# Clustering stage of an attention and cluster block: another order of the one-hot steps, and the table load moved ahead of the filler

## The chip, the cores and the metric

The kernel runs on one core of a Trainium2 chip. A core has five engines that run beside each other, each working through its own list of instructions in order: TensorE (PE in the profile, with its weight loads as PEld), VectorE (DVE), ScalarE (ACT), GpSimd (POOL) and SyncE (SP), which only starts DMA transfers here. They wait for one another by semaphores. The metric is the time of one execution on the device, in microseconds (us). Everything is computed in fp32.

## The reference

Two layers are applied to x of shape (4, 256, 64, 64): a self-attention over the 4096 positions of each image, and then a block with a group norm, a clustering, an MLP and two batch-normed products. The change lies in the clustering alone:

```python
feat, val = conv1x1(x, f_w, f_b), conv1x1(x, v_w, v_b)   # 96 channels: 4 heads of 24
xf, vf = split(feat), split(val)        # image folded 2 x 2, heads apart
cen, v_cen = pool(xf), pool(vf)         # 4 centres for each fold and head
cn, pn = cen / |cen|, pts / |pts|
sim = sigmoid(beta + alpha * cn @ pn.T)             # 4 centres x 1024 points
mask = one_hot(argmax(sim, over the centres))       # each point keeps its best centre
sim = sim * mask
agg = (sim @ v2 + v_cen) / (mask.sum(-1) + 1)
out = sim.T @ agg                                   # back to the points
```

The kernel takes the sigmoid as 0.5 tanh(half the argument) + 0.5. So for each point: a length, a scaled product, a tanh, an affine step, and a one-hot of the largest of four values, the first one where two are equal.

## The kernel before, in words

The four images are handled one after the other: attention, clustering, MLP. Their work is interleaved: while the clustering or the MLP of one image waits, matmuls of the next image's projections (or, for the last image, the rest of the one before) are put in as filler. `fill(n)` takes n such pieces from a list; a piece `v_half` is two matmuls (L314, tile vp), and after each second one ScalarE copies the result out (L322). The order on each engine is the order of the Python program: nothing is reordered afterwards.

In `cluster`, an image is cut into 8 blocks of 512 points. For each block `nb`, PE computes features, values and scaled similarities in one group of matmuls (L861, tile fv). VectorE then copies out features and values with their bias (L870, tile vf) and the similarities (L877, tile sg), and the squares of the features (L841, on GpSimd but for the last block) are summed to lengths (L842, tile prn, in `heads`).

Blocks 0 to 3 make the first row of folds, blocks 4 to 7 the second, and `f` is 0 or 1 for them. When all lengths of a row are there, `similar(f)` takes the reciprocal root (L171 on VectorE, the root L172 on ScalarE, the reciprocal L174 on VectorE), scales the similarities with it (L812, VectorE) and takes the tanh (L813, ScalarE). `largest(f)` has the affine step (L821), the largest of four (L822), a comparison (L823) and a product with a rank (L824), and `weights(f)` the largest rank (L830), the one-hot (L831) and the product of similarity and one-hot (L834, tile sim). The table `later` says where the first row's steps stand: `similar(0)` ahead of block 6, and `largest(0)` and `weights(0)` ahead of block 7, whose copies L870 and L877 thus follow them on VectorE.

ScalarE needs another function table for the root than for the tanh. `table(f)` runs one small activation on a tile `probe` (L237), by which the table is loaded at that place. In `similar` this stands behind the whole of `rsqrt`, and with it behind whatever `meanwhile` puts in: for the second row `fill(2)`, a filler piece whose copy L322 is then ahead of the load on ScalarE.

After the last block PE runs `fill(2)`, then 32 small matmuls with the pooling weights (L891, agg from pool_w), which need the values of every block, then the filler of `similar(1)` and `fill(3)`. Then it counts the points of each centre with matmuls over the one-hots (L912, tile cnt), sums the weighted values (L891, agg from sim), turns sim and the sums (L930, L939) and multiplies with the projection (L951, tile gp). The last image has its filler from the MLP of image 2's last block (L1059, L1076), with tanh-based activations of it (L1071, in `gelu`) behind each tanh.

Of the kernel before, what the change touches and what calls it, by code (L numbers as in the profile page):

```python
# [9 lines left out]
AF = mybir.ActivationFunctionType  # L10
ALU = mybir.AluOpType
AX = mybir.AxisListType
# [14 lines left out]
L2_EPS = 1e-12  # L27
# [18 lines left out]
def attention_then_cluster_block(  # L46
# [17 lines left out]
    nc = tc.nc  # L64
# [104 lines left out]
    def rsqrt(dst, src, eps, meanwhile=lambda: None):  # L169

        nc.vector.tensor_scalar(dst, src, eps, None, ALU.add)  # L171
        nc.scalar.activation(dst, dst, AF.Sqrt)  # L172
        meanwhile()
        nc.vector.reciprocal(dst, dst)  # L174
# [60 lines left out]
    def table(f):  # L235

        nc.scalar.activation(probe, probe, f)  # L237
# [455 lines left out]
    def cluster(b, ys, stats, cells, rest, fill, gelu):  # L693
# [51 lines left out]
        bests = [scr[:, f * 64 : (f + 1) * 64] for f in range(2)]  # L745
# [3 lines left out]
        oh = scr[:, NB:]  # L749
# [22 lines left out]
        for f, o in enumerate((0, 16 + 2 * ED)):  # L772
# [15 lines left out]
        prns = [small.tile([P, 64], F32, tag="prn", name=f"prn_{b}_{f}") for f in range(2)]  # L788

        sgs = [  # L790
            work.tile([P, NB // 2], F32, tag=f"w{f}", bufs=1, name=f"sg_{b}_{f}") for f in range(2)
        ]

        sim = spool.tile([P, 8, 4, 32], F32, tag="s", name=f"sim_{b}")
# [3 lines left out]
        def folded(t):  # L798
            return t.rearrange("p (q j s) -> p q j s", q=2, j=8)

        def quad(t):
            return t.rearrange("p (c m) -> p c m", m=4)

        def over_m(t):
            return t.unsqueeze(2).to_broadcast([P, 64, 4])

        def similar(f, meanwhile=lambda: None):

            sg = sgs[f]
            rsqrt(prns[f], prns[f], L2_EPS, meanwhile)  # L810
            table(AF.Gelu_apprx_tanh)
            nc.vector.tensor_tensor(quad(sg), quad(sg), over_m(prns[f]), ALU.mult)  # L812
            nc.scalar.activation(sg, sg, AF.Tanh, scale=ab[:, 0:1], bias=ab[:, 1:2])  # L813
            if f == 0:
                gelu(0)
                table(AF.Sqrt)

        def largest(f):

            sg, o, best = sgs[f], oh[:, f * 256 : (f + 1) * 256], bests[f]  # L820
            nc.vector.tensor_scalar(sg, sg, 0.5, 0.5, ALU.mult, ALU.add)  # L821
            nc.vector.tensor_reduce(best, quad(sg), AX.X, ALU.max)  # L822
            nc.vector.tensor_tensor(quad(o), quad(sg), over_m(best), ALU.is_equal)  # L823
            nc.vector.tensor_tensor(  # L824
                quad(o), quad(o), rank.unsqueeze(1).to_broadcast([P, 64, 4]), ALU.mult
            )

        def weights(f):
            sg, o, best = sgs[f], oh[:, f * 256 : (f + 1) * 256], bests[f]
            nc.vector.tensor_reduce(best, quad(o), AX.X, ALU.max)  # L830
            nc.vector.tensor_tensor(quad(o), quad(o), over_m(best), ALU.is_equal)  # L831
            own = slice(2 * f, 2 * f + 2)
            s = sim[:, :, own, :16].rearrange("p j q s -> p q j s")
            nc.vector.tensor_tensor(s, folded(sg), folded(o), ALU.mult)  # L834
        later = {6: lambda: similar(0), 7: lambda: (largest(0), weights(0))}

        def heads(nb):

# [10 lines left out]
        for nb in range(NBLK):  # L849
            fh, o = nb // 4, nb % 4  # L850
# [17 lines left out]
            for g in range(2):  # L868
                q = 2 * fh + g
# [30 lines left out]
        summed(lambda j, q: pool_w[:, j], True)  # L900
        heads(NBLK - 1)
        similar(1, lambda: fill(2))
        gelu(1)
        fill(3)
        table(AF.Sqrt)
        largest(1)
        weights(1)

        cnt_p = ps_a.tile([P, NB], F32, tag="a1", name=f"cnt_{b}")
# [632 lines left out]
    with tc.manual_schedule():  # L1542
        here = attention(0, xs0)
        here.alone()
        late = None
        for b in range(B):
            xs1, begun = [], []
            nxt = attention(b + 1, xs1) if b + 1 < B else None

            def ahead():  # L1550
                if nxt and len(xs1) < N // XT:
                    xs1.append(load_x(b + 1, len(xs1)))
                elif late and not begun:
                    begun.append(begin())

            begin, todo, gelu = late or (None, list(nxt.projections) if nxt else [], lambda i: None)
            fill = filler(todo)
            stats, cells, rest = here.weighting(ahead, fill, (lambda: None) if b else derived)
            turned = turn_w2(b, not nxt)
            stats2 = cluster(b, here.xs, stats, cells, rest, fill, gelu)  # L1560

            late = mlp(b, here.xs, stats2, fill, nxt, NBLK - (b == B - 2), turned)
            here = nxt
# [76 lines left out]
```

## Time and profile before

| | |
|---|---|
| median of 3 runs | 3378.88 us (3378.66 to 3379.28) |
| the profiled execution: its own time | 3378.26 us |
| its span, first to last instruction | 3376.5 us |
| PE, DVE, ACT, POOL busy | 98%, 66%, 50%, 57% of the span |
| mean granted clock of PE | 0.996 of full speed |
| the chain that ended last | PE 94%, DVE 4%, ACT 1% |

The profile is of one execution; times within it are us from the first instruction. A busy share is time in which an engine had an instruction running. The granted clock is the share of its full speed at which PE was allowed to run. The chain that ended last is followed back from the last instruction, at each step to what released it or to the instruction before it on its engine. A view of waits puts an engine's idle time down to the instruction that released it. In all views L12 is line 12 of the kernel.

### The profile page before, as it was taken

To read this page: it belongs to the slowest core of one execution; us is meant where nothing else is said; L and a number is where in the kernel's file an instruction comes from. 1 tells how busy PE (TensorE), PEld (TensorE's weight loads), DVE (VectorE), ACT (ScalarE), POOL (GpSimd) and SP (SyncE) were. 2 spreads that over 40 slices of the span, in tenths; PEclk is the share of its full clock that TensorE was granted. 3 is DMA by queue.
4 is the path that set the end of the run, shared out by engine and by line. 5 is a ranking of instruction groups with operands and counts; after the bars stand their busy time and mean duration, and the time that the engine had idled before them with its cause. 6 is when DMAs were issued, how large, how long until landed. Compare 5 with 4: busy or idle time off the path is not lost.

```text
span 3376.5 us, 34772 instructions
## 1 busy us (share of the span) xinstructions
PE 3318.5 (98%) x12322; PEld 1815.5 (54%) x12322; DVE 2226.3 (66%) x3546; ACT 1687.1 (50%) x2253; POOL 1929.7 (57%) x1366
## 2 busy tenths in 40 slices
PE   8999999999999999999999999999999999999999
PEld 4434445788533444578843334457873344346686
DVE  5667664677666766467766676646766766764675
ACT  5545543445555554345555555434555555544444
POOL 2655666366365666536645566554644676573664
PEclk9999999999999999999999999999999999999999
DMA  2000002000000000100000000020000000010000
GB/s 71 13 13 11 16 7 86 4 13 19 25 13 13 13 13 22 70 4 19 14 29 13 10 13 13 22 71 4 20 26 13 13 13 13 10 39 1 13 20 26
DMA packets 43102, 70.99 MB, mean 21 GB/s; under 512 B 9680, under 2 KB 18480, under 8 KB 42928
## 3 DMA queue, kind: packets, MB, share of 16 engines
q1 hardware_dynamic: 38064, 61.94, 5.5%
q10 hardware_dynamic: 4608, 6.30, 0.8%
q8 instruction: 97, 1.59, 0.2%
q14 instruction: 77, 0.63, 0.1%
q0 software_dynamic: 256, 0.52, 0.1%
HBM read 43.46 MB, written 16.89 MB: 18 GB/s over the span
## 4 chain that ended last, share of the span: by engine, by line
PE 94%; DVE 4%; ACT 1%; POOL 0%; issue 0%; DMA 0%; SPq 0%; ACTq 0%; POOLq 0%; DVEq 0%
PE av L477 53%; PE mo L1278 10%; PE sc L363 8%; PE hq L1361 5%; PE hp L1361 3%; PE hr L1361 3%; PE vp L314 2%; PE fv L861 2%; PE mo L1262 1%; PE hq_pw L1361 1%; PE pw L1215 1%; PE hr_pw L1361 1%; PE op L982 1%; PE hp_pw L1361 1%; PE qp L333 0%; PE kp L291 0%
## 5 line engine op out<-in xcount | busy, mean ns | idle before, releaser
L477 PE MATMUL av<-s,v 128*128 128x512 f32 x4096 | 1819.2, 598 | 0.6 <-ACT s L467 0.6
L472 POOL TENSOR_TENSOR acc<-acc,s 128x1024 f32<-128x1024 f32 x448 | 1057.1, 2360 | 538.3 <-ACT s L467 519.5
L477 PEld LDWEIGHTS av<-s,v 128*128 128x128 f32 x4096 | 759.0, 190 | 1044.8 <-issue 1034.5
L467 ACT ACTIVATE s<-s 128x1024 f32<-128x1024 f32 x512 | 541.0, 1059 | 591.1 <-DVE s L464 550.2
L464 DVE TENSOR_TENSOR s<-s,mb 128x1024 f32<-128x1024 f32 x512 | 595.8, 1206 | 18.4 <-ACT mb L448 16.7
L385 DVE TENSOR_TENSOR top<-sc,top 128x1024 f32<-128x1024 f32 x196 | 239.4, 1222 | 374.7 <-PE sc L363 374.6
L1316 ACT ACTIVATE hs<-hs,pv_s 128x256 f32<-128x256 f32 x496 | 233.3, 505 | 339.2 <-DVE hs L1352 339.2
L1278 PE MATMUL mo<-hs,w 128*128 128x256 f32 x1512 | 387.9, 382 | 0.0
L381 ACT COPY s<-sc 128x1024 f32<-128x1024 f32 x224 | 225.1, 1005 | 225.6 <-PE sc L363 225.6
L1278 PEld LDWEIGHTS mo<-hs,w 128*128 128x128 f32 x1512 | 282.0, 190 | 60.2 <-ACT hs L1316 19.9
L363 PE MATMUL sc<-q,k 32*128 32x512 f32 x2048 | 299.9, 640 | 0.4 <-ACT s L386 0.4
L388 DVE TENSOR_TENSOR top<-sc,top 128x1024 f32<-128x1024 f32 x196 | 240.1, 1225 | 72.6 <-ACT s L381 59.6
L386 ACT COPY s<-sc 128x1024 f32<-128x1024 f32 x224 | 227.3, 1015 | 66.0 <-DVE top L383 36.1
L1352 DVE TENSOR_TENSOR hs<-hq,hs 128x256 f32<-128x256 f32 x496 | 198.5, 421 | 75.5 <-PE hq L1361 65.2
L469 POOL TENSOR_TENSOR acc<-s 128x1024 f32<-128x1024 f32 x32 | 75.3, 2352 | 287.6 <-ACT s L467 287.6
L1285 POOL TENSOR_TENSOR hs<-hs 128x256 f32<-128x256 f32 x108 | 82.3, 762 | 194.5 <-ACT hs L1369 91.4
L363 PEld LDWEIGHTS sc<-q,k 32*128 32x128 f32 x2048 | 86.4, 182 | 183.1 <-issue 122.0
L1352 DVE TENSOR_TENSOR hs<-hp,hs 128x256 f32<-128x256 f32 x124 | 52.1, 420 | 143.0 <-ACT hs L1369 143.0
L1361 PE MATMUL hr<-xn,w 128*128 128x256 f32 x496 | 127.5, 379 | 0.5 <-DVE hs L1352 0.5
L314 PE MATMUL vp<-wv_s,x 128*128 128x256 f32 x512 | 123.4, 387 | 0.2 <-ACT v L322 0.2
L314 PEld LDWEIGHTS vp<-wv_s,x 128*128 128x128 f32 x512 | 93.5, 190 | 25.5 <-issue 10.5
L1361 PEld LDWEIGHTS hr<-xn,w 128*128 128x128 f32 x496 | 94.1, 190 | 19.1 <-issue 4.8
(261 smaller groups left out, 3528.0 us busy)
## 6 DMA issues: line engine op xcount, KB each, us to landing
x<-in_x SPq DMA_DIRECT2D x32, 512.0 KB, 6.7
out<-xn SPq DMA_DIRECT2D x62, 256.0 KB, 2.1
w<-in_w SPq DMA_DIRECT2D x8, 1024.0 KB, 10.7
mr<-row_mx SPq DMA_DIRECT2D x28, 256.0 KB, 3.1
rden<-row_rd SPq DMA_DIRECT2D x28, 256.0 KB, 3.1
q<-q ACTq DMA_DIRECT2D x96, 64.0 KB, 2.0
mix<-in_wfv SPq DMA_DIRECT2D x8, 192.0 KB, 8.4
q<-q SPq DMA_DIRECT2D x24, 64.0 KB, 2.1
```

The lines of the kernel that those rows point to most:

```text
L314: nc.tensor.matmul(vps[0][:, i % 2, :], xs[i * P // XT][:, k, o : o + P], wv_s[:, k, :], start=(k == 0), stop=(k == KC - 1),)
L363: nc.tensor.matmul(halves[r // 2][:, r % 2, :], k_s[rows, g, :], q_s[rows, :], start=True, stop=True)
L385: nc.vector.tensor_tensor(top, halves[1], top, ALU.max)
L388: nc.vector.tensor_tensor(top, halves[0], top, ALU.max)
L464: nc.vector.tensor_tensor(sh, sh, mxs[nb].unsqueeze(1).to_broadcast([P, 2, NB]), ALU.subtract)
L467: nc.scalar.activation(sh, sh, AF.Exp)
L472: nc.gpsimd.tensor_tensor(acc, acc, s[:, 2 * h : 2 * h + 2], ALU.add)
L477: nc.tensor.matmul(av[c], own["v"][:, RG * g + quarter, c * P : (c + 1) * P], slots[u][:, quarter, :], start=(g == 0 and quarter == 0), st ...
L1278: return nc.tensor.matmul(bank[:, half * HB : (half + 1) * HB], a[:, j], t, start=start, stop=stop)
L1316: nc.scalar.activation(src, src, AF.Gelu_apprx_tanh, bias=pvc("b1", P, j + 4 * (i > 1)))
L1352: nc.vector.tensor_tensor(dst, ps, term, ALU.add)
L1361: nc.tensor.matmul(out, w, x, start=True, stop=True)
```

## The change

`largest` and `weights` are cut anew. The affine step becomes a function of its own, `affine(f)`. `largest(f)` now goes up to the one-hot, and `weights(f)` has only the last product. Ahead of block 7 there is only `affine(0)`. The first row's one-hot comes after `similar(1)`, its filler and its table loads in the program; on VectorE it follows the scaling of the second row's similarities directly. Then come the second row's affine step and one-hot, and at the end both products. In `similar`, the table of the tanh is asked for between the root and the filler of `meanwhile`.

```diff
-            rsqrt(prns[f], prns[f], L2_EPS, meanwhile)
-            table(AF.Gelu_apprx_tanh)
+            def between():
+                table(AF.Gelu_apprx_tanh)
+                meanwhile()
+
+            rsqrt(prns[f], prns[f], L2_EPS, between)
...
+        def affine(f):
+            nc.vector.tensor_scalar(sgs[f], sgs[f], 0.5, 0.5, ALU.mult, ALU.add)
+
         def largest(f):
             sg, o, best = sgs[f], oh[:, f * 256 : (f + 1) * 256], bests[f]
-            nc.vector.tensor_scalar(sg, sg, 0.5, 0.5, ALU.mult, ALU.add)
             nc.vector.tensor_reduce(best, quad(sg), AX.X, ALU.max)
             nc.vector.tensor_tensor(quad(o), quad(sg), over_m(best), ALU.is_equal)
             nc.vector.tensor_tensor(
                 quad(o), quad(o), rank.unsqueeze(1).to_broadcast([P, 64, 4]), ALU.mult
             )
-
-        def weights(f):
-            sg, o, best = sgs[f], oh[:, f * 256 : (f + 1) * 256], bests[f]
             nc.vector.tensor_reduce(best, quad(o), AX.X, ALU.max)
             nc.vector.tensor_tensor(quad(o), quad(o), over_m(best), ALU.is_equal)
-            own = slice(2 * f, 2 * f + 2)
-            s = sim[:, :, own, :16].rearrange("p j q s -> p q j s")
-            nc.vector.tensor_tensor(s, folded(sg), folded(o), ALU.mult)
-        later = {6: lambda: similar(0), 7: lambda: (largest(0), weights(0))}
+
+        def weights(f):
+            s = sim[:, :, 2 * f : 2 * f + 2, :16].rearrange("p j q s -> p q j s")
+            nc.vector.tensor_tensor(
+                s, folded(sgs[f]), folded(oh[:, f * 256 : (f + 1) * 256]), ALU.mult
+            )
+
+        later = {6: lambda: similar(0), 7: lambda: affine(0)}
...
         gelu(1)
         fill(3)
         table(AF.Sqrt)
+
+        largest(0)
+        affine(1)
         largest(1)
+        weights(0)
         weights(1)
```

## The prediction

> **What bounds the kernel now.** I read the page first: TensorE (PE) is busy 98% of the span, and the chain that ended last is 94% PE and 4% VectorE (DVE). A change on VectorE and ScalarE (ACT) can matter only where PE waits for them. So next the waits of PE over the whole run (engine, line and what it waited for: us in total, times, longest):
>
> ```profile
> PE cnt L912 <- DVE scr L831: 9.9, 4, 2.7
> ...
> PE agg L891 <- DVE vf L870: 2.1, 8, 0.3
> ```
>
> The first row is PE's longest wait of all, and the diff reorders the very instruction named, L831, the last step of the one-hot. It occurs once per image: 2.71 us in images 0, 1, 2 and 1.74 in image 3. The second row is the copy-out of the last features. Then the chain through image 1's wait (start us, length us, what):
>
> ```profile
> 1450.06 0.65 DVE sg L821
> ...
> 1453.44 0.47 DVE vf L870
> ...
> 1454.01 0.47 DVE vf L870
> 1454.48 0.04 issue
> 1454.53 0.52 PE agg L891 x10
> 1455.04 1.94 PE vp L314 x8
> 1457.00 0.59 ACT v L322
> 1457.61 1.28 ACT L237
> 1458.90 0.20 ACT probe L237
> 1459.11 0.50 ACT sg L813
> ...
> 1462.26 2.82 PE cnt L912 x16
> ```
>
> The chain winds through three engines: the first row's one-hot (L821 to L834) delays the last features (L870), these delay the pooling matmuls (L891) and the filler matmuls behind them (vp), the filler's copy (L322) stands ahead of the table load, the load ahead of the tanh (L813), and the second row's one-hot comes last. The timeline has the idle times (start, length, what, idle before it and its releaser):
>
> ```profile
> 1454.97 4.58 PE L314 MATMUL vp<-wv_s,x 128*128 128x256 f32 x20
> 1462.26 2.82 PE L912 MATMUL cnt<-scr,ones 128*96 128x64 f32 x16 [2.71 <-DVE scr L831]
> ...
> 1457.22 0.42 DVE L812 TENSOR_TENSOR sg<-sg,prn 128x256 f32<-128x256 f32 x1
> 1459.63 0.29 DVE L821 TENSOR_SCALAR sg<-sg 128x256 f32<-128x256 f32 x1 [1.99 <-ACT sg L813]
> ```
>
> VectorE idles 1.99 us for the tanh just when PE is about to run out of filler. Last, busy time by stretches of 3.41 us, laid on the moments at which PE's granted clock changes (each engine's busy us and count, then the clock, DMA share, GB/s):
>
> ```profile
> 1458.64:1462.05 3.41, 0.92 (x5) 0.46 (x3) 2.25 (x6) 2.90 (x6) 0.00 (x0) 1.00 0.00 0
> 1462.05:1465.47 3.42, 3.21 (x28) 3.09 (x32) 0.90 (x4) 0.00 (x0) 0.00 (x0) 0.50 0.00 0
> 1465.47:1468.88 3.41, 3.41 (x66) 3.12 (x59) 0.67 (x2) 0.24 (x1) 0.00 (x0) 0.50 0.00 0
> ```
>
> PE was busy 0.92 us of the first stretch, and its clock is 0.50 in the next two: the wait is paid a second time, as slow matmuls behind it.
>
> [...] all drops and returns lie on one grid of 3.413 us (625.75, 1462.05, 2301.7, 3114.1), [...] stretches with PE busy 0.70, 0.92, 1.38 and 1.67 us (the four counting waits) were followed by half clock, stretches with 1.76 (from 3144.80) and 1.82 us (from 1492.77) were not. [...] the load here is 1283 ns, but the probe starts 0.02 us after it, so I use 1.28 + 0.20. [...]
>
> **The change, part by part (image 1; images 0 and 2 have the same intervals within 0.02 us).**
> 1. Six DVE instructions (L822, L823, L824, L830, L831, L834) leave the place ahead of the last L870. They stand at 0.457 us start to start, and move L870 from 1453.36 to about 1450.73. It cannot go earlier: its matmuls (L861) end about 1450.7, the earlier blocks being copied out every 2.82 us (1442.25, 1445.07). The affine L821 stays put; its end, 1450.70, falls together with that. Gain 2.63 us for everything on DVE up to L812: 1457.22 becomes 1454.59. GpSimd's square for the block before (L841, until 1450.42) is ready.
> 2. The pooling matmuls no longer wait. 52 of 64 records took 1.35 us, so all take 1.66, from 1452.31 to 1453.97, where the filler began at 1454.97: 1.00 us earlier. Filler then ends at 1458.55 instead of 1459.55, its first copy L322 starts at 1456.00.
> 3. The table load follows the square root. The root starts at 1456.34 - 2.63 = 1453.71 (the copy ahead of it ends at 1453.01), load and probe until about 1455.4, before PE delivers: the 1.48 us are hidden behind the matmuls. The tanh now waits only for the copy: 1456.50, against 1459.01. If that cover were gone, the tanh would lose up to 1.5 us.
> 4. Five DVE instructions of the first row come in behind L812: 1454.59 + 0.46 + 5 x 0.457 = 1457.34. The tanh lets DVE go at 1456.50 + 0.62 (1459.01 to 1459.63 before) = 1457.12. So DVE is now last, by 0.2 us. Affine and five steps take 1459.63 to 1462.26 = 2.63 before, hence counting starts at 1459.97: **2.29 us earlier**, and PE's wait is 1.42 us.
> 5. The two weight products (2 x 0.46) go behind the one-hots; counting takes PE at least 1.55 us, which hides them. Nobody else waits for them. No DMA, no SP or GpSimd instruction moves.
> Image 3 has no copy ahead of the tanh: L812 at 3108.66 - 2.63 = 3106.03, first row done at 3108.78, which replaces 3110.09: 1.31 us, wait 1.44. Sum of the shifts: 3 x 2.29 + 1.31 = **8.2 us**.
> 6. The clock. With at most 1.44 us idle, a stretch keeps at least 1.97 us busy, above the edge between 1.67 and 1.76, so half clock should vanish from the four places. From counting to the gp matmul (L951) it took 5.76, 7.23, 5.73, 5.73 us. At full clock: counting 1.55 (2300.32 to 2301.87), 64 records of agg 1.66 (as in 2), then 1.22 (629.74 to 630.96 of image 0): 4.43. Savings 1.33 + 2.80 + 1.30 + 1.30 = **6.7 us**. Unknown is whether small matmuls count as busy: if they do not, this is 0; if they do, 6.7. I take 6.7, because at half clock the stretch 625.75 to 629.16, made of counting and agg alone, brought the clock back.
> Sum 14.9 us. Against the profiled execution (3378.26, span 3376.5) that is 3363.4; the runs' median is 0.6 above, so 3364.0.
>
> **Rivals.**
> A (forecast): both terms, **3364.0**, own range 3361.5 to 3367.5; 0.50.
> B: the shift comes, but the clock falls in most places, since the stretch around the wait holds mostly 64-column matmuls. For it: image 3's stretch had only 1.74 us idle, and 1.38 of its 1.67 busy were counting. Against it: the return at 629.16. 3378.9 - 8.2 = 3370.7, with partial cases from 3367.5; 0.27.
> C: the filler does not come earlier (the pooling has another floor), so copy at 1457.00, tanh 1457.50, DVE 1458.12: 1.51 x 3 + 1.31 = 5.8 us, clock still falling: 3373.1, or 3372 to 3378 with further losses; 0.15. That the reordering does nothing is part of it: against it, L831 is named on PE's chain.
> D, the other side: the same grid bites elsewhere. At the start of each MLP PE idles in short pieces (stretch from 1492.77: busy 1.82, barely above the edge), and at the end of the attention hand-over (busy 1.98 from 2533.80). Everything behind moves against the grid. A stretch that falls costs up to 1.7 us, half of 3.41. To end slower than before under B's 8.2 us, five such stretches must fall; eleven places at most would give 3378.9 - 8.2 + 18.7 = 3389. Three runs within 0.62 us speak against such swings; 0.08 together with what I overlooked.
>
> **How the numbers follow.** Likeliest is A. The range reaches from 3361.0 (0.4 us per image more, from DVE slots that close up) to 3373.0, taking in A, B and the upper part of C; some 0.2 is left out. A measurement of this kernel tells about 0.2%, 6.8 us: faster is below 3372.1 (A, B, a little of C, 0.80), the same up to 3385.6 (most of C and part of D, 0.14), slower 0.06.
>
> **What would show it.** Right: L870 of the last block starts about 0.0 us after its matmuls; no PE wait at pooling; in images 0 to 2 the table load starts within 0.05 us of the root; DVE has no idle before the second affine; PE waits 1.4 us for counting, 5.7 in sum instead of 9.9; granted clock 1.00 behind it; counting to gp 4.4 us. Wrong: an idle DVE before the second affine (then the copy is the floor, C), a clock of 0.50 behind counting (B), or new half-clock stretches in the MLP starts (D).

## The result, and the profile after

The changed kernel takes 3362.7 us (median of 6 runs, 3361.72 to 3363.63) against 3379.05 us (6 runs, 3377.62 to 3379.28): ratio 0.9953, 95% interval 0.9944 to 0.9963, or 16 us. The forecast was 3364.0, range 3361.0 to 3373.0. The profiled execution took 3361.72, with a span of 3359.9 us against 3376.5.

In the view of PE's waits over the whole run, the row that led the list has moved to third place:

```profile
PE kp L291 <- DMA x<-in_x: 9.7, 3, 8.7
PE tt L399 <- DVE top L393: 7.0, 3, 3.9
PE cnt L923 <- DVE scr L834: 5.4, 4, 1.4
```

The counting (L912 before, L923 now) waits 5.4 us instead of 9.9 in sum. The row of the pooling matmuls waiting for the last features, 2.1 us before, is gone altogether.

The chain through image 1's wait (start us, length us, what) is now VectorE alone, but for one root:

```profile
1446.82 0.55 DVE vf L877
...
1449.58 0.20 DVE prn L171
1449.79 0.02 issue
1449.81 0.27 ACT prn L172
1450.07 0.02 issue
1450.10 0.56 DVE prn L174
1450.66 0.02 issue
1450.68 0.43 DVE sg L816
1451.11 0.34 DVE scr L828
...
1452.85 0.42 DVE scr L834
1453.27 0.21 DVE sg L823
...
1455.33 0.43 DVE scr L834
1455.77 0.04 issue
1455.81 1.57 PE cnt L923 x16
```

The copy-out of the last features (L877, before L870) follows the affine step L823 at once. Filler, filler's copy, table load and tanh have left the chain. The timeline of the same place (start, length, what; PE, then ScalarE, then VectorE) shows where they went:

```profile
1448.44 1.53 PE L898 MATMUL agg<-vf,pool_w 128*32 128x96 f32 x64
1449.89 4.58 PE L314 MATMUL vp<-wv_s,x 128*128 128x256 f32 x20
1455.81 1.57 PE L923 MATMUL cnt<-scr,ones 128*96 128x64 f32 x16 [1.33 <-DVE scr L834]
...
1450.08 1.28 ACT L237 ACT_TABLE_LOAD   x1
1451.38 0.20 ACT L237 ACTIVATE probe<-probe 128x1 f32<-128x1 f32 x1
1451.92 0.58 ACT L322 COPY v<-vp 128x512 f32<-128x512 f32 x1 [0.34 <-PE vp L314]
1452.41 0.60 ACT L817 ACTIVATE sg<-sg,ab 128x256 f32<-128x256 f32 x1
...
1453.19 0.28 DVE L823 TENSOR_SCALAR sg<-sg 128x256 f32<-128x256 f32 x1
```

All pooling matmuls (32 instructions, which show as 64 records) run without a gap. The load is over before PE delivers the filler that ScalarE copies, the tanh follows, and the second affine has no idle time ahead of it, where it had 1.99 us. Last, the stretch of the clock's grid in which image 1's wait lies and the next (busy us and count of PE, PEld, DVE, ACT, POOL, then the granted clock):

```profile
1452.60:1456.01 3.41, 2.08 (x11) 1.52 (x10) 3.20 (x10) 2.48 (x4) 0.00 (x0) 1.00 0.02 5
1456.01:1459.42 3.41, 3.41 (x86) 3.19 (x86) 1.41 (x5) 0.24 (x1) 0.00 (x0) 1.00 0.00 0
```

The clock stays at 1.00. From counting to the gp matmul it takes 4.18 us in every image.

Two intervals that can be read in any trace of this kernel serve for all that follows, image by image: S, from the end of the last L861 group (L868 after) to the start of counting, holds the shift; K, from counting to the gp matmul, holds the clock.

| kernel | S, images 0 to 3 | PE's wait | K, images 0 to 3 |
|---|---|---|---|
| before | 11.61, 11.61, 11.61, 10.62 | 2.71 x 3, 1.74 | 5.76, 7.22, 5.73, 5.73 |
| after | 9.03, 9.03, 9.04, 9.03 | 1.33 to 1.37 | 4.18, 4.19, 4.18, 4.19 |

S falls by 3 x 2.58 + 1.59 = 9.3 us and K by 24.45 - 16.74 = 7.7 us, together 17.0; the spans differ by 16.6. The remaining 0.4 lies outside S and K. The largest piece of it is ahead of them: in image 0 the last L868 group ended at 614.17 us where the last L861 group had ended at 613.59. This point lies between 613.59 and 614.97 in the twelve traces of this document, so a difference of 0.6 us there is within the scatter of single executions.

### The profile page after: what moved, and what is told of

The parts are those of the page before. It is cut to its first block, busy times and chain, and to the rows that moved or that the text cites. A ratio compares the mean times of both kernels' runs of the same rounds, so it can differ in the third digit from the quotient of the medians.

```text
span 3359.9 us, 34780 instructions
## 1 busy us (share of the span) xinstructions
PE 3308.0 (98%) x12322; PEld 1807.2 (54%) x12322; DVE 2225.8 (66%) x3546; ACT 1683.6 (50%) x2253; POOL 1930.0 (57%) x1366
## 3 DMA queue, kind: packets, MB, share of 16 engines
q8 instruction: 97, 1.59, 0.2%
## 4 chain that ended last, share of the span: by engine, by line
PE 94%; DVE 5%; ACT 1%; issue 0%; POOL 0%; DMA 0%; SPq 0%; ACTq 0%; POOLq 0%; DVEq 0%
PE av L477 53%; PE mo L1289 10%; PE sc L363 8%; PE hq L1372 5%; PE hp L1372 3%; PE hr L1372 3%; PE vp L314 2%; PE fv L868 2%; PE mo L1273 1%; PE hq_pw L1372 1%; PE pw L1226 1%; PE hr_pw L1372 1%; PE op L993 1%; PE hp_pw L1372 1%; PE qp L333 0%; PE kp L291 0%
```

## The experiments

All ratios are to the kernel before, measured on the same chip beside it. Line numbers are each kernel's own.

**Without the table move.** The reordering alone:

```diff
-            rsqrt(prns[f], prns[f], L2_EPS, between)
+            rsqrt(prns[f], prns[f], L2_EPS, meanwhile)
+            table(AF.Gelu_apprx_tanh)
```

> The changed kernel with the table load put back behind the filler: only the reordering is left. Theory 1 (the shift and the clock both count): in images 0 to 2 the tanh again waits for copy, load and probe, 1.48 us more, VectorE idles about 1.3 us before the second affine, PE's wait for counting becomes about 2.7 us and the clock falls to 0.50 behind it. Time 3362.7 + 3 x 1.35 + 3 x (1.3 to 2.8) = 3370.7 to 3375. Theory 2 (shift alone counts, the clock costs nothing): 3362.7 + 4.1 = 3366.8. Theory 3 (the table move is hidden by the filler): 3362.7.

Measured: 3368.86 us, ratio 0.9973 (0.9963 to 0.9983). The timeline of image 1, ScalarE and then VectorE:

```profile
1454.72 0.58 ACT L322 COPY v<-vp 128x512 f32<-128x512 f32 x1 [1.86 <-PE vp L314]
1455.33 1.28 ACT L237 ACT_TABLE_LOAD   x1
1456.62 0.20 ACT L237 ACTIVATE probe<-probe 128x1 f32<-128x1 f32 x1
1456.73 0.59 ACT L813 ACTIVATE sg<-sg,ab 128x256 f32<-128x256 f32 x1
...
1457.35 0.29 DVE L819 TENSOR_SCALAR sg<-sg 128x256 f32<-128x256 f32 x1 [1.28 <-ACT sg L813]
```

S is 10.4 in images 0 to 2 and 9.03 in image 3: the mechanism as expected, 1.37 us an image, with VectorE idle for 1.28. So the load is not hidden by the filler (theory 3 falls). PE's wait is 2.71 us again, and K is 5.61, 7.07, 4.19, 4.19. That image 2 kept its clock behind a wait of 2.71 us was not expected. The traced execution is the slowest of the eight, 3371.30 us, and lies inside theory 1's 3370.7 to 3375; six of the others lie between 3368.46 and 3369.30, below it. The median is 6.2 us above the changed kernel's 3362.7, and the shift takes 4.1 of that; the 2 us left are less than two falls of the clock at 1.4 us each (5.61 against 4.19), where three had been expected (by the ratios it is 6.8 us in all, and the same holds). Which images kept the clock in those runs was not traced.

**The table move alone**, in the kernel before: the edit to `similar` of the change and nothing else.

> The kernel before with the table load alone moved ahead of the filler. Theory 1: the root still comes late, so load and probe end at 1458.0 of the old timeline, one us after the filler's matmuls; the tanh gains only 0.5 us in images 0 to 2 and nothing in image 3, PE's wait stays at 2.2 us and the clock still falls: 3379.0 - 1.5 = 3377.5. Theory 3 (the load is what the tanh waited for): 3 x 1.48 and full clock, about 3379.0 - 4.4 - 5.4 = 3369.

Measured: 3374.99 us, ratio 0.9991 (0.9984 to 0.9997), a gain of 3.0 us (1 to 5.4). S fell by 0.51 in images 0 to 2 and by less than 0.01 in image 3, as worked out: the root comes so late in the old order that load and probe end at 1457.96, when the filler has long been delivered (its copy started at 1457.00 in the kernel before). Nearly all of the rest is the clock: image 1 lost one half-clock stretch instead of two (K 5.73, not 7.22). The expectation had left that out, and the time is lower by it. So alone the parts bring 3.0 us and, from the run before, about 9; together 16. Together they bring more than the sum, since only the early root lets the load end before the filler (in image 1 of the changed kernel load and probe end at 1451.58, and the copy starts at 1451.92), and only both bring all four waits to 1.4 us.

**The clock alone.** Matmuls that nobody reads fill PE's wait in the kernel before:

```diff
         cnt_p = ps_a.tile([P, NB], F32, tag="a1", name=f"cnt_{b}")
+        for _ in range(3 if b == B - 1 else 5):
+            nc.tensor.matmul(
+                cnt_p[:, C:], wv_s[:, 0, :P], wv_s[:, 1, :], start=True, stop=True
+            )
```

> The kernel before, with matmuls that nobody reads put into PE's wait for counting: five of 128x256 (about 2.3 us) in images 0 to 2, three (1.4 us) in image 3. Counting starts when it did, so the shift is nil and only the clock is changed. Theory 1: granted clock 1.00 behind the wait, counting to gp 4.4 us instead of 5.7 to 7.2, time 3379.0 - 6.7 = 3372.3. Theory 2 (the clock costs nothing on this path): 3379.0 or a little more.

Measured: 3371.27 us, ratio 0.9979 (0.9971 to 0.9988): 7.1 us faster by adding work. Image 1 on PE:

```profile
1459.11 2.32 PE L911 MATMUL cnt<-wv_s 128*128 128x256 f32 x10
1461.98 1.57 PE L916 MATMUL cnt<-scr,ones 128*96 128x64 f32 x16 [0.55 <-DVE scr L831]
1463.48 1.53 PE L891 MATMUL agg<-vf,sim 128*32 128x96 f32 x64
```

S is 11.60 to 11.61 and 10.62, the same as before; K is 4.18 to 4.19 in all images. The counting matmuls take 1.57 us (2.82 before), the sums 1.53 (2.79 before). The clock is thus a cost of its own, and it makes 7.1 of the 16 us; what is left, 9.3, is the fall of S.

**The control.** The changed kernel with two such matmuls in its shorter wait.

> The changed kernel with two such unread matmuls (0.9 us) in its shorter wait of about 1.35 us in each image. The control of the run before: if the shorter wait already keeps the clock up, they change nothing, 3362.7; if some clock was still lost, or if busy matmuls help or hurt in another way, the time moves by over 1 us.

Measured: 3362.68 us, ratio 0.9953 (0.9938 to 0.9968), S and K as in the changed kernel. Nothing is left to be had from the clock there, and in these four runs (3361.68 to 3363.64) the added matmuls show no other effect.

**How much room is left.** One or two extra VectorE reductions between the first row's one-hot and the second affine, in the changed kernel; the second kernel has `range(2)` in place of `range(1)`:

```diff
         largest(0)
+        for _ in range(1):
+            nc.vector.tensor_reduce(bests[0], quad(oh[:, :256]), AX.X, ALU.max)
         affine(1)
```

> The changed kernel with one extra VectorE reduction, whose result nobody reads, between the first row's one-hot and the second affine: counting 0.46 us later in each image, PE's wait about 1.8 us. Theory 1 with the edge at 1.7 us idle in a stretch of 3.41: 3362.7 + 1.8 = 3364.5 where the wait is split by the grid, and up to 1.3 us more for each image where it is not, at most 3370. Theory 2 (no cost of the clock): 3364.5.

> The same with two extra reductions: counting 0.91 us later, PE's wait about 2.3 us. Theory 1: 3362.7 + 3.7 = 3366.4, and the clock falls in most images, 1.3 us or more each: 3370 to 3373. Theory 2: 3366.4, twice the step of one reduction and no kink.

One: 3363.07 us, ratio 0.9959 (0.9945 to 0.9972); S 9.48 to 9.49, wait 1.79 to 1.82, K 4.18 to 4.19 in all images. Two: 3367.44, ratio 0.9975 (0.9964 to 0.9986), with runs up to 3374.76; S 9.94, wait 2.24 to 2.27, K 4.18, 4.18, 5.77, 4.18. Each reduction moves counting by its 0.46 us at once: VectorE does set the start of counting. With one the clock held everywhere, which both theories allowed at 3364.5, so this run doesn't tell them apart. Theory 1's edge of 1.7 us idle was my estimate from stretches of the kernel before (1.74 us idle lost the clock, 1.65 kept it). With two it fell, in the traced execution, in one image only, and four of the seven runs are lower than the 3370 to 3373 of theory 1. The other three (3370.15 to 3374.76) were not traced.

**When the clock falls.** Theory 1 had expected more falls than came. Between the first 20 and the last 8 us of the kernel before, the granted clock goes to 0.50 at 625.77, 1462.03, 2301.71, 2540.64, 3114.08 and 3137.98 us and comes back 3.41 or 6.83 us later; in that of the changed kernel it goes at 2527.80 and 3121.72. All these moments lie multiples of 3.413 us apart within each trace, and so do the falls worked out from stretches of 0.2 us in four experiments (reordering alone: 626.58, 1459.43, 2534.63; table move alone: 626.74, 1463.01, 2299.28, 3111.64; one reduction: 2528.54, 3122.46; two: 2292.26, 2531.19, 3128.52, 3135.35). Below, the first line of each pair is a stretch of this grid, the second the one after, whose granted clock (the third number from the end) shows whether it fell. The kernel before, image 3:

```profile
3110.69:3114.10 3.41, 1.67 (x17) 1.38 (x16) 2.26 (x6) 2.93 (x5) 0.00 (x0) 1.00 0.00 0
3114.10:3117.52 3.42, 3.42 (x70) 3.03 (x69) 0.99 (x3) 0.24 (x1) 0.00 (x0) 0.50 0.02 5
```

One extra reduction, image 0:

```profile
620.49:623.90 3.41, 1.62 (x10) 1.11 (x9) 3.20 (x10) 2.07 (x3) 0.00 (x0) 1.00 0.00 0
623.90:627.31 3.41, 3.41 (x86) 3.19 (x86) 1.30 (x4) 0.29 (x2) 0.00 (x0) 1.00 0.02 5
```

The reordering alone, image 0 and then image 2:

```profile
623.17:626.58 3.41, 1.99 (x40) 1.92 (x44) 2.28 (x7) 0.73 (x2) 0.00 (x0) 1.00 0.00 0
626.58:630.00 3.42, 3.42 (x60) 3.13 (x50) 0.82 (x3) 0.68 (x2) 0.00 (x0) 0.50 0.02 5
...
2295.70:2299.11 3.41, 2.25 (x52) 2.19 (x56) 2.31 (x7) 0.46 (x2) 0.00 (x0) 1.00 0.00 0
2299.11:2302.52 3.41, 3.38 (x57) 2.58 (x45) 0.61 (x3) 1.74 (x4) 0.00 (x0) 1.00 0.02 5
```

With 1.67 us busy the clock fell, with 1.62 it held. In the last two PE ran counting and sums alone: behind 1.99 us busy the clock fell, behind 2.25 it held. So no single edge of busy time fits the stretches as they are cut here. And a wait of 2.71 us that the grid cuts into 1.55 and 1.16, as in image 2 here (1.86 and 2.25 us busy), was harmless in both halves.

The stretches differ in what PE ran: of the 1.67 us, 1.38 were counting, and of the 1.62, 1.32 were filler of 256 columns. Why the clock fell behind the one and held behind the other, no run here shows.

A wait of 1.33 us followed within its stretch by counting and sums alone would leave 2.08 us busy (an estimate, 3.41 less 1.33). That lies between 1.99, where the clock fell, and 2.25, where it held, and what the clock would do is open. No image of the changed kernel lay so in its trace: the stretches with the waits had 2.05 to 2.12 us busy, most of it filler.

**A step further.** In the changed kernel VectorE idles 0.32 us for the root and is last by 0.16 us. The first edit issues the tanh ahead of the filler's copy, the second also puts the first row's first reduction into the wait for the root:

```diff
-        similar(1, lambda: fill(2))
+        similar(1, lambda: top(0))
+        fill(2)
```

The diff shows the second edit, without the lines that make the first reduction of `largest(f)` a function `top(f)`; the first edit has `similar(1)` instead.

> The changed kernel itself once more, to stand beside the next two on one chip: ratio 0.9953 to the kernel before.

> The changed kernel with only the tanh issued ahead of the filler's copy on ScalarE. In the changed kernel VectorE reaches the second affine last, 0.16 us after the tanh would let it go, so an earlier tanh is worth nothing: the same time within 0.5 us, and PE's wait stays at 1.33 us. If the filler's copy were the floor (rival C), counting would come up to 0.9 us earlier in images 0 to 2.

> A try at more: the first row's first reduction put between the second row's square root and its reciprocal, where VectorE idles 0.32 us, and the tanh issued ahead of the filler's copy on ScalarE. VectorE sets the start of counting, so it comes 0.3 us earlier in each image: 3362.7 - 1.3 = 3361.4. If the filler's copy or the tanh were the floor instead, the gain in images 0 to 2 would be over 0.5 us each or nothing.

> The kernel with the first row's first reduction in VectorE's wait for the root and the tanh ahead of the copy, beside the changed kernel on one chip. From its trace counting comes 0.45 us earlier in each of four images: 1.8 us faster than the changed kernel, ratio 0.9947 to 0.9948 to the kernel before.

Side by side: the changed kernel 3362.62 us, ratio 0.9955 (0.9942 to 0.9969); the tanh first 3361.47, 0.9952 (0.9940 to 0.9965); with the reduction 3360.74, 0.9950 (0.9937 to 0.9962), and on another chip 3359.91, 0.9947 (0.9934 to 0.9959). The tanh alone leaves S at 9.03 to 9.04 and PE's wait at 1.34 to 1.37, so the copy was not the floor; the ratios don't tell these two apart. With the reduction, S is 8.58 in all four images, 0.45 less. VectorE:

```profile
1449.64 0.20 DVE L171 TENSOR_SCALAR prn<-prn 128x64 f32<-128x64 f32 x1
1449.75 0.41 DVE L823 TENSOR_REDUCE scr<-sg 128x64 f32<-128x256 f32 x1
1450.16 0.55 DVE L174 RECIPROCAL prn<-prn 128x64 f32<-128x64 f32 x1
```

The reduction fits into the wait and the reciprocal follows without idle. Beside the changed kernel all five runs (3360.02 to 3361.17) lie below all five of its (3361.43 to 3364.12). The medians differ by 1.9 us, where 1.8 were expected, though the intervals of the ratios overlap. From the kernel with the tanh alone the median differs by 0.7 us only. Between the first and the last counting its trace is 1.54 us shorter than that kernel's, where 3 x 0.45 = 1.35 were to come; but its first counting started 0.26 us later, since the work ahead of S had ended 0.73 us later.

## Why the prediction was right, step by step

**Step 1, the last features earlier: right.** L877 starts 0.04 us after the modelled end of its matmuls (1446.78 to 1446.82).

**Step 2, the pooling: right, a little small.** 64 records took 1.45 us to the start of the filler, not 1.66 (the 1.35 us of 52 records from which 1.66 was scaled up run to the modelled end of the last one; here that end, 1449.97, lies 0.08 us behind the start of the next matmul, 1449.89), so the filler came 1.21 us earlier against the end of the last features' matmuls instead of 1.00.

**Step 3, the load behind the root: right, and the experiments show that it carries its part.** The estimate of 1.5 us if its cover were gone measured 1.37 us an image with the move undone.

**Step 4, VectorE last: right in kind, 0.28 to 0.29 us too small in each image.** VectorE goes on to the second affine without idle, with 0.16 us to spare (0.2 forecast). The forecast shift was 2.29 and 1.31, measured 2.58 and 1.59. Most of it is the term of the slots: I took 0.457 us for every step. Two instructions that don't need their predecessor's result started 0.34 to 0.35 us after it, L828 behind L816 (1450.68 to 1451.03) and the affine behind the one-hot (1452.85 to 1453.19). That is 0.23 us. The prediction had named it, "DVE slots that close up", only for the lower end.

**Step 5, the products behind: right.** Both end at 1456.42, while counting runs until 1457.38.

**Step 6, the clock: right in size and in outcome, but its reason is not secured.** 6.7 us were forecast, K fell by 7.7; the run with filled waits has 7.1. Too small was the gain, since 4.43 was taken for K at full clock and 4.18 measured; of the 0.25 the sums are most, 1.46 us from their start to the next matmul against the 1.66 taken over from step 2. The sentence that a stretch with 1.97 us busy lies safely above an edge between 1.67 and 1.76 does not hold for stretches cut as the prediction cut them: one with 1.99 us busy, all of it small matmuls, fell. The edge was my estimate from the kernel before, and the experiments show no such edge: 1.62 us busy kept the clock, 1.99 lost it. The waits of 1.33 to 1.37 us lay in stretches with 2.05 to 2.12 us busy, most of it dense filler; why the clock held behind them was not shown. The return of the clock at 629.16, on which I relied, came behind a stretch without any idle time (3.41 us busy of 3.41), and so could not show what a partly idle one does.

**The sum.** 14.9 us were forecast and 16.35 measured (medians): shift 8.2 against 9.3, clock 6.7 against 7.7, less 0.4 elsewhere, by the traces (16.6 between the spans).

**The rivals.** B is refuted for the cases traced: K is 4.18 to 4.19 in all images. C is refuted: the filler came earlier, and an earlier tanh did not move counting. D did not come: while PE works, the clock is below 1.00 in the changed kernel only where the kernel before has it too, behind PE's wait of 3.95 us for VectorE (L393) and at the last MLP start (from 2527.8 and 3121.7).

## What to carry to other kernels

A wait in front of a serial piece was worth cutting here although the engine is 98% busy (9.3 us by the shift), and in image 1 before, the price of a wait on PE was twice its length (2.71 us of waiting and 3.04 us more behind it, 7.22 against 4.18): look at the granted clock behind it, not only at the idle time. Filling such a wait with useless matmuls told the two apart in one run (7.1 us for the clock). The two moves brought more together (16 us) than the sum of each alone (3.0 and about 9), since one took away the other's floor; follow the chain through all engines before judging one alone.

## What the runs showed of the hardware

In the six traces named above, the half clock came and went at moments that lie multiples of 3.413 us apart within one execution. In stretches of this length the full clock was kept with 1.62 us busy, 1.32 of it 256-column filler (one extra reduction, image 0), and with 2.25 us of 64-column counting and 96-column sums (reordering alone, image 2), and lost with 1.99 us of the latter (reordering alone, image 0); the cause is open. Behind a wait of 2.71 us the clock held in one image of the reordering alone, where the grid cut the wait into 1.55 and 1.16 us, and fell in two. With two extra reductions a wait of 2.24 to 2.27 us cost the clock in one image of four. The shortest wait for counting behind which it fell was 1.74 us (kernel before, image 3).

At half clock the 16 counting matmuls took 2.82 us and the 64 records of the sums 2.79 us (kernel before, image 1), against 1.57 and 1.53 at a granted clock of 1.00 (the same kernel with its waits filled).

On VectorE, in image 1 of the changed kernel, the steps from L828 to L834, each of which reads the result of the one before, stood 0.44 to 0.46 us start to start. L828 started 0.35 us after L816 and L823 0.34 after L834, whose results they don't read.
